# Block products in seven (Strassen's scheme) for two matrix products of a four-layer graph kernel, softmax steps moved forward, and layer 2 cut into pieces

## The chip, the cores and the metric

The kernel runs on one core of a Trainium2 chip. The metric is the device time of one execution in microseconds (us). Engines: PE is TensorE's matmuls, PEld its weight loads, DVE is VectorE, ACT is ScalarE, POOL is GpSimd.

## The reference, cut to what matters

`x` has shape (128 batches, 128 nodes, 256 features); `adj` is 128 x 128; all is fp32. Four layers follow one another, each wrapped in `x = layernorm(x + layer(x))`.

```python
# layer 0: graph attention over 512 edges (src, dst), 4 heads
Xq = (H @ W_lin.T).reshape(bt, n, h, dh)          # "queries"
Xv = (H @ W_val.T).reshape(bt, n, h, dh)
e  = einsum(leaky_relu(Xq[:, src] + Xq[:, dst]), a) + log(A0[src, dst] + EPS)
attn = softmax of e over the edges with the same src      # segment max, exp, sum
Y  = segment_sum(attn * Xv[:, dst], src) @ W_out.T
# layer 1: three products with weights, each mixed over nodes with adj * adj
h = relu(mix(x @ W1)); h = relu(mix(h @ W2)); out = mix(h @ W3)    # widths 512, 1024, 256
# layer 2: three matrices adj_0 (diagonal), adj_1, adj_2 (triangles), each with its own W[k]
# layer 3: mix, x @ W1.T, batch norm over all rows, relu, @ W2.T, batch norm
```

## The kernel before

The batches go in 32 groups of four. The main loop is a software pipeline: in repetition `k`, layer 2 and the first half of layer 3 work on group `a = k-1`, layer 1 on `c = k`, the end of layer 0 and the start of layer 1 on `b = k+1`, scores and softmax on `e = k+2`, and queries and values on `g = k+3`. Each engine's instructions stand in the order of the program, and the DVE lines in the prediction show DVE working them off in that order (a scaled copy at 1003.51, the three passes of a score from 1003.85, a sum at 1007.50, the next scaled copy at 1008.09). Layer 1's second product and layer 3's hidden product are already done in seven block products.

Queries and values of one batch are two matmuls of 512 columns, eight in a group; layer 1's first product has the same form:

```python
def values(k, i, copy=None, queue=None):
    ...
    pq = ps("pq")
    for c in range(DC):                                   # DC = 2
        nc.tensor.matmul(pq, s.xts[i // 2][:, i % 2, c, :], wqv[:, c, :], start=(c == 0), stop=(c == DC - 1))
    nc.scalar.copy(s.qt[:, i, :], pq[:, :D])
    copy(s.xv[:, i, :], pq[:, D:])

def first(k, i):
    ...
    for dc in range(DC):
        nc.tensor.matmul(ph, s.mx[i // 2 * 2][:, i % 2, dc, :], w1_sb[:, dc, :], ...)
    nc.scalar.activation(h1, ph, AF.Relu)
```

Layer 2 of one group. `mix` makes one batch's three mixed inputs: two by matmul, copied by ACT, and the diagonal one as a scaled copy by DVE. `prod` multiplies them with the weights. `behind` is the score of chunk 0, three passes of DVE over 1024 columns:

```python
mix(0); mix(1)
...
prod(0)
mix(2)
if behind:
    behind()                     # score(e, 0)
prod(1)                          # ends with a DVE sum of batches 0 and 1
mix(3)
layer_norm(wk, s.xr[:, 0:2, :])
prod(2); prod(3)                 # prod(i) reads mix(i)
```

The softmax is a chain of two scans, a subtraction and exponential, and two more scans (`softmax_parts`, a generator). Its steps stand between the products of the hidden layer; the last one stands behind layer 0's norm, just ahead of `attention`, whose transposes on PE read it:

```python
            next(parts, None)                 # last of layer 3's hidden products, and their statistics
            next(steps, None)                 # third scan
            gather(g)
            stage_a(b)                        # W_out, sum, layer 0's norm
            next(steps, None)                 # fourth scan
            third(c, 0)
            attention(e)                      # PE transposes the softmax result
```

Of the kernel before, what the change touches and what calls it, by code (L numbers as in the profile page):

```python
# [25 lines left out]
def gnn_stack(ctx: ExitStack, tc: tile.TileContext, x, adj, w_qv_t, a, w_out_t, src, dst,  # L26
# [101 lines left out]
    with ExitStack() as phase:  # L128
# [4 lines left out]

        quads = [Quad() for _ in range(NQ)]
# [49 lines left out]
        def values(k, i, copy=None, queue=None):  # L184

            copy = copy or nc.vector.tensor_copy
            s = quads[k]
            if i == 0:
                s.qt = wk.tile([P, QB, D], F32, tag="xb", name=f"qt{k}", bufs=1)
                s.xv = ws.tile([P, QB, D], F32, tag="xv", name=f"xv{k}", bufs=3)  # L190
            pq = ps("pq")
            for c in range(DC):
                nc.tensor.matmul(pq, s.xts[i // 2][:, i % 2, c, :], wqv[:, c, :], start=(c == 0), stop=(c == DC - 1))  # L193
            nc.scalar.copy(s.qt[:, i, :], pq[:, :D])
            copy(s.xv[:, i, :], pq[:, D:])
            if i == QB - 1:
                s.qd = q_dram[k % 4]
                (queue or nc.sync).dma_start(s.qd, s.qt.rearrange("p b d -> p (b d)"))

        def gather(k, z=None):  # L200

            s = quads[k]
            s.z = z or [ws.tile([P, QB * D], F32, tag="zs", name=f"zs{k}_{c}", bufs=NE) for c in range(NE)]
            jobs = [(t, c) for t in range(2) for c in range(NE)]
            if k == 0:
                jobs = [(0, 0), (0, 1), (1, 0), (0, 2), (1, 1), (0, 3), (1, 2), (1, 3)]
            for t, c in jobs:
                idx, op = ((src_idx, ALU.bypass), (dst_idx, ALU.add))[t]
                nc.gpsimd.indirect_dma_start(out=s.z[c], out_offset=None, in_=s.qd,  # L209
                                             in_offset=bass.IndirectOffsetOnAxis(ap=idx[:, c:c + 1], axis=0),  # L210
                                             compute_op=op)
# [14 lines left out]
        def softmax_parts(k):  # L226
# [12 lines left out]
            e = wk.tile([R, E], F32, tag="e", name="e", bufs=1)  # L239
            nc.vector.tensor_sub(e, pe[:R, :], m)  # L240
            nc.scalar.activation(e, e, AF.Exp)
            yield
            nc.vector.tensor_tensor_scan(f, keep_f, e, initial=0.0, op0=ALU.mult, op1=ALU.add)
            yield
            nc.vector.tensor_tensor_scan(m[:, ::-1], keep_b[:, ::-1], f[:, ::-1], initial=0.0,
                                         op0=ALU.mult, op1=ALU.max)
            s.ex, s.den = e, m
# [21 lines left out]

        def by_row(k, j, copy=None):  # L270

            s = quads[k]
            if j == 0:
                s.adc = wk.tile([P, R, N], F32, tag="adc", name=f"adc{k}", bufs=1)
# [34 lines left out]
        def mix1(k, j):  # L309
# [8 lines left out]
            if j == 0:  # L318
                s.mx = {}
                s.h1 = {}  # L320
                s.m2 = m2_tile()
            s.mx[j] = mx

        def first(k, i):
# [7 lines left out]
            s.h1[i] = h1  # L332


# [5 lines left out]
        def m2_tile():  # L340
            return wk.tile([P, 7, 2, 2, N], F32, tag="m2", name="m2", bufs=1)

        def mix2(k, i):
# [3 lines left out]
            for c in range(K1):  # L347
                nc.tensor.matmul(pm[:, c // 2, c % 2, :], s.h1[i][:, c * P:(c + 1) * P], wt_t, start=True, stop=True)  # L348
# [13 lines left out]
        def second_sums():  # L362

            a11, a12 = w2_sb[:, :2, :512], w2_sb[:, 2:, :512]
            a21, a22 = w2_sb[:, :2, 512:], w2_sb[:, 2:, 512:]
            s1, s2, s4 = (w2_s[:, i] for i in range(3))
            nc.vector.tensor_add(s1, a21, a22)
            nc.vector.tensor_sub(s2, s1, a11)
            nc.vector.tensor_sub(a21, a11, a21)
            nc.vector.tensor_sub(s4, a12, s2)  # L370
            second.blocks = {"A11": a11, "A12": a12, "A22": a22, "S1": s1, "S2": s2, "S3": a21, "S4": s4}
# [89 lines left out]
        def third(k, j, between=None):  # L461
            s = quads[k]
            p3 = ps("p3")
            for t in range(2):
                if t and between:
                    between()
                for f in range(K2):
                    nc.tensor.matmul(p3[:, t * D:(t + 1) * D], s.h2[f // 2][:, f % 2, j + t, :], w3_sb[:, f, :],  # L468
                                     start=(f == 0), stop=(f == K2 - 1))
            s3 = temp("s3")  # L470
# [21 lines left out]
        def stage_e(k, late=None, behind=None):  # L492
# [31 lines left out]
            if late is not None:  # L524
                late_sums(late)
            prod(0)
            mix(2)
            if behind:
                behind()
            prod(1)  # L530
            mix(3)
            layer_norm(wk, s.xr[:, 0:2, :])
            prod(2)
            prod(3)
# [18 lines left out]
        def hidden_sums():  # L553

            a11, a12, a21, a22 = (l3w1[:, h, o * 256:(o + 1) * 256] for o in range(2) for h in range(2))
            s1, s2, s3, s4 = (l3w1_s[:, i] for i in range(4))
            nc.vector.tensor_add(s1, a21, a22)
            nc.vector.tensor_sub(s2, s1, a11)
            nc.vector.tensor_sub(s3, a11, a21)
            nc.vector.tensor_sub(s4, a12, s2)  # L560
            hidden.blocks = {"A11": a11, "A12": a12, "A22": a22, "S1": s1, "S2": s2, "S3": s3, "S4": s4}
# [5 lines left out]
        def hidden(k):  # L567

# [4 lines left out]
            b11, b12, b21, b22 = (s.ag[h][:, o * half:(o + 1) * half] for h in range(2) for o in range(2))  # L573
            t12 = temp("t12")
            t1, t2, t3, t4 = t12[:, :half], t12[:, half:], s.spare[0], s.spare[1]
            nc.vector.tensor_sub(t1, b12, b11)
            nc.vector.tensor_sub(t2, b22, t1)
            nc.vector.tensor_sub(t3, b22, b12)
            nc.vector.tensor_sub(t4, b21, t2)

            def product(bank, blk, rhs, new):
                for i in range(2):
                    nc.tensor.matmul(bank[:, i, :], hidden.blocks[blk][:, i * P:(i + 1) * P], rhs,
                                     start=new and i == 0, stop=i == 1, skip_group_check=True)

            def bank(name):
                return ps(name).rearrange("p (i n) -> p i n", i=2)

            def kept_copy(src_, name):
                t = temp(name).rearrange("p (i n) -> p i n", i=2)  # L590
                nc.scalar.copy(t, src_)
                return t

            def block(row, col):
                return zt[:, 2 * row:2 * row + 2, col * half:(col + 1) * half]

            def stats(row):
                for c in (2 * row, 2 * row + 1):
                    nc.vector.bn_stats(st1[:, c, k, :], zt[:, c, :])

            yield
            y = bank("y3")
            product(y, "A11", b11, True)
            p1 = kept_copy(y, "p1")
            z = bank("z3")
            product(z, "S1", t1, True)
            yield
            product(y, "S2", t2, False)
            u2 = kept_copy(y, "u2")
            x = bank("x3")  # L610
            product(x, "A12", b21, True)
            nc.vector.tensor_add(block(0, 0), x, p1)
            yield
            product(y, "S3", t3, False)
            u3 = kept_copy(y, "u3")
            nc.vector.tensor_add(block(1, 1), z, u3)
            yield
            product(y, "A22", t4, False)
            nc.scalar.copy(block(1, 0), y)
            product(z, "S4", b22, False)  # L620
            nc.vector.tensor_add(block(0, 1), z, u2)
            stats(1)
            stats(0)
# [17 lines left out]
        w1_sb = ctile([P, DC, F1], "w1", pool=cst2)  # L641
        w2_sb = ctile([P, K1, F2], "w2", pool=cst2)
# [16 lines left out]

        def iteration(k):  # L660
# [4 lines left out]
            if a > 0:  # L665
                stage_e(a, c if has_c else None, (lambda: score(e, 0)) if has_e else None)
            else:
                late_sums(c)
                score(e, 0)
                hidden_sums()  # L670
# [11 lines left out]
            if has_g and g + 1 < NQ:  # L682
                quads[g + 1].xg = load_x(g + 1, "xg", 1, ws)
            stage_f(a)
            steps = softmax_parts(e) if has_e else iter(())
# [4 lines left out]
            parts = hidden(a)  # L690
            next(parts)
            if has_g:
                values(g, 0, nc.scalar.copy)
                values(g, 1, nc.scalar.copy)
            next(parts)
            next(steps, None)
            if has_g:
                values(g, 2, nc.scalar.copy)
            next(parts)
            next(steps, None)  # L700
            if has_g:
                values(g, 3, nc.scalar.copy)
            next(parts)
            if has_b:
                aggregate(b)
            next(steps, None)
            next(parts, None)
            next(steps, None)
# [5 lines left out]
            third(c, 0)  # L714
# [3 lines left out]
            if has_b:  # L718
                third(c, 2)
                third_mix(c, 0)  # L720
                mix1(b, 0)
                third_norm(c, 0)
            else:
                third(c, 2, lambda: third_mix(c, 0))
                third_norm(c, 0)
            third_mix(c, 2)
            if has_b:
                mix1(b, 2)
                first(b, 0)
            third_norm(c, 2)  # L730
            if has_b:
                firsts(b)

        def firsts(b):
# [536 lines left out]
```

## Time and profile before

| | before |
|---|---|
| time, median | 3290.4 us (3289.6 to 3292.4, 4 runs) |
| PE busy | 3178.6 us, 97% of the span |
| DVE, ACT, POOL busy | 59%, 38%, 20% |
| one repetition of the steady loop | 90.25 us |

How to read the lines: in a timeline a line gives the start in us, the duration of the merged group, engine, line of the program, operation, output <- inputs by name, shapes, and count; a bracket at its end gives the idle time of the engine just before the group and what ended it. Durations of neighbouring PE groups overlap, since the profile models the end of a matmul (in the prediction's lines one group ends at 1003.24 + 2.75 = 1005.99, and the next starts at 1005.83); so costs are taken from starts. The list of waits gives who waited for what: total us, times, longest. The lines themselves stand in the prediction.

### The profile page before, as it was taken

The numbers are of one execution on the slowest core, as the hardware profiler recorded it, in microseconds if no ns is written. First come the engines' busy times: TensorE is split into PE (matmuls) and PEld (weight loads), VectorE is DVE, ScalarE is ACT, GpSimd is POOL, SyncE is SP. The second block draws the span as 40 slices with busy tenths as digits, with TensorE's granted clock in tenths as the row PEclk, the third lists the DMA queues.
The fourth block names the chain that finished last, engine by engine and source line by source line (L and its number), as shares of the span: only waits on it lengthen the run. The fifth ranks groups of instructions, "written<-read, shape, count | busy, mean of one in ns | idle before, by whom it ended". The sixth has DMA issues, their size and how long they took to land. (4 is left out here: it accounts for less than half of the span.)

```text
span 3287.6 us, 39593 instructions
## 1 busy us (share of the span) xinstructions
PE 3178.6 (97%) x15176; PEld 2462.7 (75%) x15176; DVE 1955.8 (59%) x3779; ACT 1236.2 (38%) x2248; POOL 653.8 (20%) x541
## 2 busy tenths in 40 slices
PE   6899999999999999999999999999999999999997
PEld 3677887777787878877777878788777778883444
DVE  6655565555556555655555565556555556337878
ACT  2333333333333333333333333333333333325668
POOL 4201222222111112222222111122222220001225
PEclk7999999999999999999999999999999999999999
DMA  7612333333332223333333322233333331004457
GB/s 222 180 48 82 103 97 103 103 97 103 84 103 86 77 82 97 98 102 103 97 103 85 102 88 81 77 97 103 97 103 97 103 85 51 20 20 173 177 184 279
DMA packets 118748, 344.75 MB, mean 105 GB/s; under 512 B 15008, under 2 KB 51744, under 8 KB 110240
## 3 DMA queue, kind: packets, MB, share of 16 engines
q0 software_dynamic: 45552, 151.55, 18.2%
q1 hardware_dynamic: 70960, 188.71, 15.9%
q8 instruction: 120, 1.97, 0.2%
q10 hardware_dynamic: 2048, 1.97, 0.2%
q14 instruction: 68, 0.56, 0.1%
HBM read 256.20 MB, written 85.98 MB: 104 GB/s over the span
## 5 line engine op out<-in xcount | busy, mean ns | idle before, releaser
L388 PE MATMUL ph<-m,w 128*128 128x256 f32 x2048 | 463.2, 379 | 0.0
L209 POOL DMA_INDIRECT zs<-qd,src_idx x124 | 121.2, 978 | 1683.2 <-DMA qd<-qt 1639.5
L468 PE MATMUL p<-w,h 128*128 128x256 f32 x2048 | 455.3, 380 | 0.0
L468 PEld LDWEIGHTS p<-w,h 128*128 128x128 f32 x2048 | 386.6, 190 | 52.6 <-issue 0.5
L388 PEld LDWEIGHTS ph<-m,w 128*128 128x128 f32 x2048 | 386.7, 190 | 51.3
L388 PE MATMUL ph<-m,w_s 128*128 128x256 f32 x1536 | 352.4, 379 | 0.0
L516 PE MATMUL po<-l2w,ms 128*128 128x256 f32 x1536 | 348.1, 380 | 1.2 <-DVE ms L508 1.2
L388 PEld LDWEIGHTS ph<-m,w_s 128*128 128x128 f32 x1536 | 291.8, 190 | 39.7
L516 PEld LDWEIGHTS po<-l2w,ms 128*128 128x128 f32 x1536 | 284.9, 190 | 36.3 <-DVE ms L508 1.4
L193 PE MATMUL pq<-wqv,xt 128*128 128x512 f32 x512 | 237.3, 599 | 0.2 <-ACT xt L181 0.2
L328 PE MATMUL ph<-w,mx 128*128 128x512 f32 x512 | 235.9, 593 | 0.9 <-ACT mx L317 0.9
L209 POOL DMA_INDIRECT zs<-qd,dst_idx x124 | 205.7, 1659 | 119.7 <-DMA zs<-qd,src_idx 96.8
L112 ACT ACTIVATE ln_sd<-ln_mv,eps 128x2 f32<-128x2 f32 x192 | 56.5, 294 | 421.2 <-DVE ln_mv L107 421.2
L265 POOL DMA_INDIRECT attd<-at,att_idx x128 | 128.1, 1001 | 416.9 <-DMA attd<-at,att_idx 294.0
L401 DVE TENSOR_TENSOR h<-ph,u 128x512 f32<-128x512 f32 x128 | 88.2, 690 | 168.9 <-PE ph L388 115.2
L481 DVE TENSOR_TENSOR xr<-xr,po 128x512 f32<-128x512 f32 x64 | 43.7, 683 | 230.1 <-PE po L479 230.1
L348 PEld LDWEIGHTS pm<-wt_t,h 128*128 128x128 f32 x1024 | 131.8, 191 | 49.6 <-issue 38.7
L395 ACT COPY u<-ph 128x512 f32<-128x512 f32 x128 | 75.1, 586 | 242.9 <-PE ph L388 242.9
L504 ACT COPY ms<-pm 128x512 f32<-128x512 f32 x128 | 74.9, 586 | 237.6 <-PE pm L502 230.9
L193 PEld LDWEIGHTS pq<-wqv,xt 128*128 128x128 f32 x512 | 93.7, 193 | 84.3 <-issue 81.3
L221 DVE TENSOR_TENSOR zs<-zs,a_bc 128x1024 f32<-128x1024 f32 x124 | 151.9, 1225 | 4.2
L222 DVE TENSOR_REDUCE es<-zs 128x16 f32<-128x1024 f32 x124 | 151.3, 1220 | 4.3
(250 smaller groups left out, 5163.4 us busy)
## 6 DMA issues: line engine op xcount, KB each, us to landing
ad<-attd SPq DMA_DIRECT2D x32, 1024.0 KB, 4.7
zd<-z SPq DMA_DIRECT2D x31, 1024.0 KB, 7.0
zl<-zd SPq DMA_DIRECT2D x62, 512.0 KB, 3.5
xr<-in_x_dram SPq DMA_DIRECT2D x32, 512.0 KB, 5.8
x3d<-xr SPq DMA_DIRECT2D x32, 512.0 KB, 2.6
x3l<-x3d SPq DMA_DIRECT2D x32, 512.0 KB, 5.0
out_dram<-x3l POOLq DMA_DIRECT2D x31, 512.0 KB, 5.2
qd<-qt SPq DMA_DIRECT2D x30, 512.0 KB, 2.6
```

The costliest lines, as they stand in the source:

```text
L193: nc.tensor.matmul(pq, s.xts[i // 2][:, i % 2, c, :], wqv[:, c, :], start=(c == 0), stop=(c == DC - 1))
L209: nc.gpsimd.indirect_dma_start(out=s.z[c], out_offset=None, in_=s.qd, in_offset=bass.IndirectOffsetOnAxis(ap=idx[:, c:c + 1], axis=0), com ...
L221: nc.vector.tensor_mul(z3, z3, a_bc.unsqueeze(1).to_broadcast([P, QB, D]))
L222: nc.vector.reduce_sum(s.es[:, c, :], z.rearrange("p (r d) -> p r d", d=DH), axis=AX.X)
L265: nc.gpsimd.indirect_dma_start(out=ad, out_offset=bass.IndirectOffsetOnAxis(ap=att_idx[:, c:c + 1], axis=0), in_=s.at[:, c, :], in_offset= ...
L328: nc.tensor.matmul(ph, s.mx[i // 2 * 2][:, i % 2, dc, :], w1_sb[:, dc, :], start=(dc == 0), stop=(dc == DC - 1))
L348: nc.tensor.matmul(pm[:, c // 2, c % 2, :], s.h1[i][:, c * P:(c + 1) * P], wt_t, start=True, stop=True)
L388: nc.tensor.matmul(bank[g][:, i].rearrange("p b n -> p (b n)"), wa[:, c, f:f + P], s.m2[:, blk_b, c].rearrange("p b n -> p (b n)"), start= ...
L395: nc.scalar.copy(to[g], y[g])
L401: nc.vector.tensor_add(block(g, row, col), bank[g], kept_[g])
L468: nc.tensor.matmul(p3[:, t * D:(t + 1) * D], s.h2[f // 2][:, f % 2, j + t, :], w3_sb[:, f, :], start=(f == 0), stop=(f == K2 - 1))
L516: nc.tensor.matmul(po[:, i % 2, :], mss[i][:, t, dc, :], l2w[:, t, dc, :], start=(n3 == 0), stop=(n3 == 3 * DC - 1))
```

## The change

Its intent: with fewer columns through PE, which is busy for 97% of the span and so bounds the kernel, and without PE's wait for the softmax, the time should fall. It has three parts.

1. Queries and layer 1's first product go in seven products of half-size blocks instead of eight, at the cost of sums on DVE and copies on ACT. In the code, `A11` to `B22` are the blocks of the two factors, `S1` to `S4` and `T1` to `T4` are sums of such blocks (those of the weights are made once, in repetition 0), `part` copies a partial result out of `y` by ACT, and `out` writes one block of the result, most often as the sum of a bank and such a copy.
2. The softmax steps come earlier: all are done before the hidden layer's statistics and layer 0's norm.
3. To fill PE while the sums of part 1 are made, layer 2 becomes a generator that is run in pieces, and layer 1's third product too. The score of chunk 0 is now issued behind `prod(1)`, the end of layer 2's third piece (`mix(0)` and `mix(1)` are the first, run a repetition earlier). Three gather buffers take the place of four; the fourth chunk is gathered behind that score.

```diff
+        class Seven:
+            def p1(self):
+                self.y = ps("y")
+                self.mm(self.y, "A11", "B11", True)
+                self.k1 = self.part(self.y, 0)
+            def p5(self):
+                self.z = ps("z")
+                self.mm(self.z, "S1", "T1", True)
+            def p2(self):
+                x = ps("x")
+                self.mm(x, "A12", "B21", True)
+                self.out(0, 0, x, self.k1)
+            def p6(self):
+                self.mm(self.y, "S2", "T2", False)
+                self.k2 = self.part(self.y, 1)
+            def p7(self):
+                self.mm(self.y, "S3", "T3", False)
+                self.k3 = self.part(self.y, 2)
+                self.out(1, 1, self.z, self.k3)
+            def p4(self):
+                self.mm(self.y, "A22", "T4", False)
+                self.out(1, 0, self.y, None)
+            def p3(self):
+                self.mm(self.z, "S4", "B22", False)
+                self.out(0, 1, self.z, self.k2)
... (sums_a, sums_b, node_blocks, node_product: each product is two matmuls of 256 columns)
@@ stage_e: layer 2
             mix(0)
             mix(1)
-            if late is not None:
-                late_sums(late)
+            yield
             prod(0)
+            yield
             mix(2)
-            if behind:
-                behind()
             prod(1)
+            yield
             mix(3)
             layer_norm(wk, s.xr[:, 0:2, :])
             prod(2)
+            yield
             prod(3)
@@ iteration: its start
+            next(parts, None)
+            next(parts, None)
+            if has_e:
                 score(e, 0)
+                gather_last(e)
+            for _ in parts:
+                pass
... (second product)
@@ iteration: queries, softmax and hidden layer
+            steps = softmax_parts(e) if has_e else iter(())
+            next(steps, None)
+            h = hidden(a, room[5:] + room[2:4])
             if has_g:
-                values(g, 0, nc.scalar.copy)
-                values(g, 1, nc.scalar.copy)
+                run(q.p1, q.p5, q.p2)
+                next(steps, None)
+                q.p6()
+            run(h.p1, h.p5)
             next(steps, None)
             if has_g:
-                values(g, 2, nc.scalar.copy)
+                q.p7()
+            run(h.p2, h.p6)
             next(steps, None)
             if has_g:
-                values(g, 3, nc.scalar.copy)
+                run(q.p4, q.p3)
+                spill(g)
+            next(steps, None)
+            h.p7()
             if has_b:
                 aggregate(b)
+            run(h.p4, h.p3)
+            hidden_stats(a)
... (layer 0's end; third product)
@@ iteration: layer 1's first product
+            mix1(b, 0)
+            mix1(b, 2)
+            third_mix(c, 0)
+            next(rest)                        # a quarter of the third product
+            w = first_seven(b)
+            third_norm(c, 0)
+            next(rest)
+            run(w.p1, w.p5, w.p2)
+            next(rest)
+            w.p6()
+            next(rest, None)
+            w.p7()
+            third_mix(c, 2)
+            w.p4()
+            w.p3()
+            third_norm(c, 2)
+            quads[c].layer2 = stage_e(c)
+            next(quads[c].layer2)
```

## The prediction

One paragraph of the recorded text is cut where it is marked. No term of the forecast's sum stood in it: the terms still add up to -35.6 us, and 3290.7 - 35.6 = 3255 us. The durations behind the added work beside PE are those of the trace before: sums on DVE of 256 and 512 columns take 425 ns (L576) and 692 ns (L612), copies on ACT 0.37 to 0.38 us (L194, L195) and 0.59 us (L591), the table load 1.28 us (L241). "DVE's FIFO as traced" means the order of the DVE lines shown there, with 3.65 us of scoring ahead of the copy that PE wants.

> **What bounds the kernel now.** I read the head of the page first, then TensorE's waits, then the timelines of TensorE (PE) and VectorE (DVE) over one repetition of the steady loop. The head of the page:
>
> ```profile
> PE 3178.6 (97%) x15176; PEld 2462.7 (75%) x15176; DVE 1955.8 (59%) x3779; ACT 1236.2 (38%) x2248; POOL 653.8 (20%) x541
> PE   6899999999999999999999999999999999999997
> ```
>
> PE is busy nearly everywhere, and DVE, the next engine, has 40% to spare. So only two things pay: fewer columns through PE, and PE's remaining waits. The list of PE's waits names the largest one:
>
> ```profile
> PE pat L255 <- DVE m L245: 32.0, 31, 1.9
> PE py L289 <- ACT adc L275: 9.9, 1, 9.9
> PE pe L231 <- DVE es L224: 9.6, 1, 9.6
> ```
>
> The first comes once per group of four batches: the transposes of the softmax result wait for its last scan. The others come once, before the loop. Stage F (L547) of successive repetitions starts 90.25 us apart (946.90, 1037.15, 1127.40 us); of these PE idles only 0.99. From the PE timeline:
>
> ```profile
> 1003.24 2.75 PE L516 MATMUL po<-l2w,ms 128*128 128x256 f32 x12
> 1005.83 1.03 PE L502 MATMUL pm<-split_t,xr 128*128 128x256 f32 x4
> 1006.70 0.38 PE L507 MATMUL pt<-ident,xr 128*128 128x128 f32 x2
> 1006.91 5.34 PE L516 MATMUL po<-l2w,ms 128*128 128x256 f32 x24
> 1012.10 5.34 PE L388 MATMUL ph<-m,w 128*128 128x256 f32 x24
> ...
> 1038.93 3.60 PE L193 MATMUL pq<-wqv,xt 128*128 128x512 f32 x8
> 1042.37 1.03 PE L583 MATMUL y<-ag,l3w 128*128 128x256 f32 x4
> ...
> 1066.23 0.42 PE L255 MATMUL pat<-ident,m 16*128 16x16 f32 x4 [0.99 <-DVE m L245]
> ```
>
> Starts give costs; durations overlap. Eight records of 512 columns take 1042.37 - 1038.93 = 3.44 us. Each program matmul is two records (512 records here for 32 x 8 matmuls), so one costs 0.860 us. In layer 1's second product, 24 records of 256 columns take 5.18 us (1012.10 to the next group's 1017.28): 0.432 us per matmul. Cost follows columns. The weight load (190 ns a record) fits under a 256-column record (216 ns), so halving the width costs nothing.
>
> DVE in the same stretch:
>
> ```profile
> 1003.51 0.42 DVE L508 TENSOR_TENSOR ms<-pt,diag_bc 128x256 f32<-128x256 f32 x1 [2.00 <-PE pt L507]
> 1003.85 1.22 DVE L219 SCALAR_TENSOR_TENSOR zs<-zs 128x1024 f32<-128x1024 f32 x1
> 1005.10 1.23 DVE L221 TENSOR_TENSOR zs<-zs,a_bc 128x1024 f32<-128x1024 f32 x1
> 1006.36 1.22 DVE L222 TENSOR_REDUCE es<-zs 128x16 f32<-128x1024 f32 x1
> 1007.50 0.68 DVE L520 TENSOR_TENSOR xr<-xb,po 128x512 f32<-128x512 f32 x1
> 1008.09 0.42 DVE L508 TENSOR_TENSOR ms<-pt,diag_bc 128x256 f32<-128x256 f32 x1
> ```
>
> DVE works here in the program's order: layer 2's scaled copy of batch 2, the whole score of one chunk (3.65 us), the sum of batches 0 and 1, the scaled copy of batch 3. That copy ends at 1008.51; PE wants it for batch 3's product at 1006.91 + 2.59 = 1009.50. There is a margin of one microsecond.
>
> [...]
>
> **The change part by part.**
>
> *Seven block products.* Queries and layer 1's first product each go from 8 matmuls of 512 columns (8 x 0.860 = 6.88 us) to 7 x 2 of 256 (14 x 0.432 = 6.04): 0.84 saved. Queries change for groups 4 to 31 (28; the start keeps the plain form), the first product for groups 1 to 31 (31). 59 x 0.84 = 49.6 us, all on PE and so on the path.
>
> *Softmax earlier.* The last scan now comes before the hidden layer's statistics and layer 0's norm. Counting with row durations from the end of the second product: scans at 2.5, 6.0, 11.0 and 12.8 us, the last done near 14, while its transposes are due near 26.6. The 0.99 us wait goes in 29 repetitions: 28.7 us.
>
> *Added work beside PE.* Per repetition two times four sums of 256 columns (1.7 us) and three sums of 512 (2.07): 7.5 us more DVE. ScalarE: eight copies of 0.375 become four of 0.586, and three copies of 0.586 are added: 1.1 us more. DVE goes from 51.2 in 88.3 us to an estimated 66%. No new bound, but new places where PE can wait. In the queries' chain I find none: S1 is ready near 1.2 us, its product due at 3.1; the narrowest point (q.p3, which needs z read, behind the exponential's 1.28 us table load) has some 0.3 us. In layer 1's chain, S1 is ready 1 us early; the last ReLU comes some 0.1 us before the mixing that reads it, because layer 2's first two mixes stand between. I allow 0.1 us a repetition, 3 us.
>
> *Layer 2 cut into pieces.* This is where I expect a new wait. score(e,0) stood between mix(2) and prod(1) on DVE; now it stands after prod(1). So DVE first waits for prod(1)'s end (call it 0), adds at 0.27 (the same lag as 1012.10 to 1012.37 in the traces), starts scoring at 0.86, finishes at 4.51, and only then makes batch 3's scaled copy, until 4.93. PE: mix(3) 1.08, prod(2) 2.59, so prod(3) is due at 3.67 and starts near 4.98. New wait: 1.31 us, in repetitions 2 to 29 (28): 36.7 us. Before, DVE used its idle time during prod(1) for the score.
>
> *Edges.* The last three repetitions have no queries between the hidden layer's products, and p7 follows p6 directly: it waits for ScalarE's copy, some 0.85 us each. Repetition 0 loses its waits at the transposes (4.39 + 1.89) in part and gets a wait before mix2. Net about +3.
>
> Sum: -49.6 - 28.7 + 36.7 + 3 + 3 = -35.6; 3290.7 - 35.6 = 3255 us. The steady period should be about 88.9 us, from 90.25.
>
> **The rivals.** *No new wait* (PE comes late to prod(3) for another reason, or DVE reaches the score in time): then -49.6 - 28.7 + 6, 3218 us, 2.2% faster. For it: the author plainly placed pieces to fill gaps. Against it: the program order, and DVE's FIFO as traced. *DVE becomes the bound in stretches*: nodes' sums, norms and ReLUs of one chain queue behind each other, and PE loses another half to one microsecond in the queries or in layer 1: 3270 to 3285 us. For it: margins of 0.1 to 0.3 us; against it: 34% of DVE stays free. *Transfers*: the fourth chunk's gather is issued only after score 0, with three buffers in place of four. It is issued some 14 us before its score is due, when the transfer engines are nearly idle (DMA share 0.11 in the second product, 0.94 where gathers now crowd), so I expect nothing.
>
> **Range and chances.** The main term I doubt is the 36.7 us. All of it away: 3218. Half a microsecond more per repetition: 3271. So 3228 to 3272 in 8 of 10. Over 2% faster needs under about 3226 us: 0.16, nearly all from the first rival. Slower by 2% would take 4 us a repetition: 0.02.
>
> **What would show it.** Stage F's starts 88.9 us apart, not 90.25 and not 87.6; the wait at the pat transposes gone; a wait of PE at layer 2's product on DVE's scaled copy, 1.3 us in 28 repetitions; records of L193 and of the first product replaced by twice 14 matmuls of 256 columns per repetition at 0.432 us. Wrong would be: that new wait absent, or PE waits at the S1, p3 or p7 products, or at mix2, above 0.3 us per repetition, or waits on the gathers' transfers.

## The result, and the profile after

The changed kernel takes 3252.2 us (median; 3249.8 to 3254.3, 4 runs) against 3290.4. The ratio is 0.9883 (95% interval 0.9865 to 0.99): 1.2% less.

The head of the page after, and the largest entries in the list of PE's waits after:

```profile
PE 3137.4 (96%) x15884; PEld 2590.5 (80%) x15884; DVE 2145.3 (66%) x4200; ACT 1276.3 (39%) x2229; POOL 644.1 (20%) x541
```

```profile
PE po L666 <- DVE ms L658: 33.9, 29, 1.5
PE pe L356 <- DVE es L349: 10.7, 1, 10.7
```

PE is busy for 41 us less (waiting changes this figure too: e1 does the same 15884 records in 3127.3 us), DVE has gone to 66%. The wait at the softmax transposes (31 times) is gone from the top, and a wait at layer 2's product (L666) on DVE's scaled copy (L658) stands there, of the same size. PE's timeline of the steady loop shows all three parts of the change:

```profile
1028.33 1.03 PE L280 MATMUL y<-wqv,xt 128*128 128x256 f32 x4
1029.20 1.03 PE L280 MATMUL z<-wqv,m 128*128 128x256 f32 x4
...
1052.97 0.41 PE L379 MATMUL pat<-ident,f 16*128 16x16 f32 x4
1053.24 0.40 PE L379 MATMUL pat<-ident,m 16*128 16x16 f32 x4
...
1066.67 1.03 PE L280 MATMUL y<-w_s,adc 128*128 128x256 f32 x4
1067.57 1.12 PE L629 MATMUL po<-s,wt_t 128*128 128x512 f32 x2
1068.53 1.03 PE L280 MATMUL y<-w_s,mx 128*128 128x256 f32 x4
...
1082.27 1.03 PE L652 MATMUL pm<-split_t,xr 128*128 128x256 f32 x4
...
1083.35 2.76 PE L666 MATMUL po<-l2w,ms 128*128 128x256 f32 x12
1087.26 2.86 PE L666 MATMUL po<-l2w,ms 128*128 128x256 f32 x12 [1.16 <-DVE ms L658]
1089.95 5.34 PE L535 MATMUL ph<-m,w 128*128 128x256 f32 x24
```

A block product of the queries takes 0.87 us from start to start. The second softmax transposes follow the first with no bracket. And prod(3), due at 1083.35 + 2.59 = 1085.94, starts at 1087.26, 1.32 us late. DVE in the same stretch says why:

```profile
1079.87 0.42 DVE L658 TENSOR_TENSOR ms<-pt,diag_bc 128x256 f32<-128x256 f32 x1 [1.19 <-PE pt L657]
1082.54 0.69 DVE L670 TENSOR_TENSOR xr<-xb,po 128x512 f32<-128x512 f32 x1 [2.24 <-PE po L666]
1083.14 1.22 DVE L344 SCALAR_TENSOR_TENSOR zs<-zs 128x1024 f32<-128x1024 f32 x1
...
1085.65 1.22 DVE L347 TENSOR_REDUCE es<-zs 128x16 f32<-128x1024 f32 x1
1086.79 0.41 DVE L658 TENSOR_TENSOR ms<-pt,diag_bc 128x256 f32<-128x256 f32 x1
```

DVE stood idle for 2.24 us until prod(1) had ended, then summed, then scored for 3.65 us, and only then made the copy that PE wanted. Before the change the scoring filled that idle time (1003.85 to 1007.58, with the sum next at 1007.50, in the prediction's lines).

Where the 35.4 us between the two profiled spans (3287.6 and 3252.2) went: the stage F starts of repetitions 1 and 29 are 2527.18 us apart before and 2488.70 after, 38.5 us less (the steady period falls from 90.25 to 88.89). The rest of the span is 3.1 us longer, which says little: in e1 and e9, two runs of one kernel, that rest is 761.65 and 766.22 us.

### The profile page after: what moved, and what is told of

The parts are those of the page before. It is cut to its first block, busy times and chain, and to the rows that moved or that the text cites. A ratio compares the mean times of both kernels' runs of the same rounds, so it can differ in the third digit from the quotient of the medians.

```text
span 3252.2 us, 41204 instructions
## 1 busy us (share of the span) xinstructions
PE 3137.4 (96%) x15884; PEld 2590.5 (80%) x15884; DVE 2145.3 (66%) x4200; ACT 1276.3 (39%) x2229; POOL 644.1 (20%) x541
## 5 line engine op out<-in xcount | busy, mean ns | idle before, releaser
L616 PE MATMUL p<-w,h 128*128 128x256 f32 x2048 | 462.3, 379 | 0.0
L666 PE MATMUL po<-l2w,ms 128*128 128x256 f32 x1536 | 355.7, 382 | 33.9 <-DVE ms L658 33.9
L666 PEld LDWEIGHTS po<-l2w,ms 128*128 128x128 f32 x1536 | 282.7, 190 | 78.7 <-DVE ms L658 45.4
L329 POOL DMA_INDIRECT zs<-qd,dst_idx x123 | 192.5, 1565 | 258.2 <-DMA zs<-qd,src_idx 246.9
L344 DVE SCALAR_TENSOR_TENSOR zs<-zs 128x1024 f32<-128x1024 f32 x123 | 149.5, 1215 | 2.4 <-DMA zs<-qd,dst_idx 2.4
L120 DVE TENSOR_SCALAR xr<-xr,ln_mv,ln_rs 128x256 f32<-128x256 f32 x384 | 145.1, 420 | 6.9
L105 DVE BATCH_NORM_STATS2 ln_st<-xr 128x6 f32<-128x256 f32 x384 | 144.2, 417 | 5.5
L477 DVE TENSOR_TENSOR h<-z,adc 128x512 f32<-128x512 f32 x62 | 41.9, 675 | 153.9 <-ACT adc L471 153.8
L640 POOL TENSOR_TENSOR xb<-xr,bias 128x512 f32<-128x512 f32 x64 | 81.6, 1275 | 293.1 <-DVE xr L120 155.2
```

Source lines behind the costliest of these rows:

```text
L105: nc.vector.bn_stats(st[:, i, :], r[:, i, :])
L120: nc.vector.tensor_scalar(r[:, i, :], r[:, i, :], mv[:, i, 0:1], rs[:, i:i + 1], op0=ALU.subtract, op1=ALU.mult)
L329: nc.gpsimd.indirect_dma_start(out=s.z[c], out_offset=None, in_=s.qd, in_offset=bass.IndirectOffsetOnAxis(ap=idx[:, c:c + 1], axis=0), com ...
L344: nc.vector.scalar_tensor_tensor(z, z, SLOPE, z, op0=ALU.mult, op1=ALU.max)
L616: nc.tensor.matmul(p3[:, t * D:(t + 1) * D], s.h2[f // 2][:, f % 2, j + t, :], w3_sb[:, f, :], start=(f == 0), stop=(f == K2 - 1))
L640: nc.gpsimd.tensor_add(s.xb[:, j:j + 2, :], xj, bias.unsqueeze(1).to_broadcast([P, 2, D]))
```

## The experiments

The theory is that of the prediction: the gain is an eighth of the columns and the softmax wait, and half of it is given back by the place of one score in DVE's queue. Rivals: DVE is simply fuller (66%), and the wait would come up anywhere; the block form itself costs less or more than its columns; the gather of the last chunk matters. Each kernel was correct. They ran on three chips (e1 to e4, e5 to e7, e8 and e9), each with the kernel before beside them (medians 3290.8, 3291.3 and 3293.4 us); the ratios are to these. The steady period is read from stage F's starts, and is what the runs are compared by below.

| run | time, median us | ratio to before (95%) | steady period us |
|---|---|---|---|
| before | 3290.4 | 1 | 90.25 |
| changed | 3252.2 | 0.9883 (0.9865 to 0.9900) | 88.89 |
| e1 changed, score forward | 3213.2 | 0.9764 (0.9748 to 0.9780) | 87.47 |
| e2 before, score late | 3329.4 | 1.0119 (1.0102 to 1.0136) | 91.67 |
| e3 before, softmax ahead | 3256.6 | 0.9896 (0.9880 to 0.9913) | 89.10 |
| e4 before, half-width matmuls | 3293.1 | 1.0010 (0.9993 to 1.0028) | 90.33 |
| e5 changed, plain queries | 3276.5 | 0.9949 (0.9932 to 0.9965) | 89.72 |
| e6 changed, node sums twice | 3261.4 | 0.9908 (0.9892 to 0.9925) | 89.13 |
| e7 changed, score behind mix(3) | 3215.3 | 0.9765 (0.9749 to 0.9781) | 87.47 |
| e8 changed, plain first product | 3272.0 | 0.9936 (0.9920 to 0.9953) | 89.58 |
| e9 as e1, another chip | 3215.5 | 0.9758 (0.9742 to 0.9775) | 87.47 |

### e1: the score forward again, in the changed kernel

```diff
             mix(2)
+            yield
             prod(1)
             yield
```

(In repetition 0, where layer 2 runs without a score, one more `next(parts)` keeps the old order.)

> The changed kernel, with one more stop in layer 2's pieces so that the score of chunk 0 stands between mix(2) and prod(1) again, as in the kernel before; all else as changed. Theory (the order in VectorE's queue makes the wait at batch 3's product): the wait of PE on the scaled copy (33.9 us in 29 times in the changed kernel) goes, the start of batch 3's product moves forward by 1.32 us in 28 repetitions, steady period 88.89 - 1.32 = 87.57 us, time 3252 - 37 = 3215 us, 0.977 of before. Rival (VectorE simply has 7.5 us more work per repetition and the wait would come up elsewhere): the wait moves to another product, period stays within 0.3 us of 88.89 and the time above 3243 us.

Measured: 3213.2 us, ratio 0.9764, period 87.47. PE and DVE of this kernel at the same place:

```profile
1066.99 5.35 PE L666 MATMUL po<-l2w,ms 128*128 128x256 f32 x24
```

```profile
1063.86 1.22 DVE L344 SCALAR_TENSOR_TENSOR zs<-zs 128x1024 f32<-128x1024 f32 x1
...
1066.37 1.22 DVE L347 TENSOR_REDUCE es<-zs 128x16 f32<-128x1024 f32 x1
1067.51 0.68 DVE L670 TENSOR_TENSOR xr<-xb,po 128x512 f32<-128x512 f32 x1
1068.10 0.42 DVE L658 TENSOR_TENSOR ms<-pt,diag_bc 128x256 f32<-128x256 f32 x1
```

prod(2) and prod(3) run as one group of 24 records (L666) without a bracket, and the copy is ready at 1068.52, some 1.1 us before prod(3) is due (1066.99 + 2.59 = 1069.58). DVE does exactly the same work, so the rival of a full DVE falls. The gain is a little larger than expected, 1.42 us per repetition and not 1.32, since the group behind the wait is slower too: its 12 records took 2.69 us (1087.26 to 1089.95), and 12 without a wait take 2.59. Why is not shown, but the same 0.10 stands behind the shorter delays of e6 and e8 below.

### e2: the score late, in the kernel before

```diff
-            if behind:
-                behind()
             prod(1)
+            if behind:
+                behind()
```

> The kernel before, with nothing changed but the score of chunk 0 issued after prod(1) in place of ahead of it. Theory (order alone): PE gains a wait at batch 3's product of about 1.3 us in repetitions 2 to 29, period 90.25 + 1.31 = 91.56, time 3290.5 + 37 = 3327 us. Rival (the wait needs the added VectorE work of the seven-product form): no new wait, within 5 us of before.

Measured: 3329.4 us, ratio 1.0119, period 91.67, which is 1.42 longer. PE's waits of this kernel:

```profile
PE po L516 <- DVE ms L508: 33.6, 29, 1.2
PE pat L255 <- DVE m L245: 31.4, 31, 1.9
```

The new wait stands beside the old one, with none of the block products' sums on DVE. The order alone makes it, and it is worth the same 1.42 us in both kernels. So the changed kernel carried a loss of about 28 x 1.42 = 40 us that its other parts made up for.

### e3: the softmax ahead, in the kernel before

```diff
             parts = hidden(a)
             next(parts)
+            next(steps, None)
             if has_g:
                 values(g, 0, nc.scalar.copy)
...
             next(parts)
+            next(steps, None)
             if has_b:
                 aggregate(b)
-            next(steps, None)
             next(parts, None)
-            next(steps, None)
             if has_g:
                 gather(g)
```

> The kernel before, with nothing changed but each softmax step one or two places earlier, so that the last scan comes ahead of the hidden layer's statistics and layer 0's norm. Theory: the 0.99 us wait at the softmax transposes goes in 29 repetitions, period 89.26, time 3290.5 - 29 = 3261.5 us. Rival (earlier scans and exponential delay the copies that the hidden layer's products wait for): part of it comes back as waits at those products, time above 3275 us.

Measured: 3256.6 us, ratio 0.9896, period 89.10. PE's timeline of this kernel at the softmax transposes:

```profile
1054.99 0.41 PE L255 MATMUL pat<-ident,e 16*128 16x16 f32 x4
1055.26 0.39 PE L255 MATMUL pat<-ident,m 16*128 16x16 f32 x4
```

The edit does not do quite what the expectation says. The first three scans move up, the third ahead of the statistics, but the fourth and last stays behind layer 0's norm in the program. It still comes in time: the second transposes, which read it, start at 1055.26 with no bracket (above), and PE's wait for it falls from 32.0 us in 31 times to 2.3 in 2. So the run shows what the wait is worth, and not the changed kernel's own order, in which the last scan (1038.80) does come ahead of the statistics (1043.44).

The wait is gone and nothing took its place. The gain is 1.15 us per repetition, more than the 0.99 listed. The transposes show it: here the second group starts 0.27 us after the first; with the wait it started at 1066.23, 1.40 after the first (1064.83), which is 1.13 more. The bracket counts only from the modelled end of the group before (0.41 us after its start), not from the moment when PE could have started the next, 0.27 us after that start in this run.

### e4: the same columns in half-width matmuls, in the kernel before

```diff
-                nc.tensor.matmul(pq, s.xts[i // 2][:, i % 2, c, :], wqv[:, c, :], start=(c == 0), stop=(c == DC - 1))
+                for hf in range(2):
+                    nc.tensor.matmul(pq[:, hf * D:(hf + 1) * D], s.xts[i // 2][:, i % 2, c, :],
+                                     wqv[:, c, hf * D:(hf + 1) * D], start=(c == 0 and hf == 0), stop=(c == DC - 1),
+                                     skip_group_check=True)
```

(And the same in `first`.)

> The kernel before, with every 512-column matmul of the queries and of layer 1's first product issued as two of 256 columns with a weight load each: the same columns, twice the instructions. Theory (cost follows columns, the weight load of 190 ns hides under a record of 216): 64 x 8 x (2 x 0.432 - 0.860) = +2 us, time 3290 to 3295 us. Rival (twice the weight loads or the instructions cost something, so that the block form gains less than an eighth): 10 percent on 6.88 us in 64 uses, +44 us.

Measured: 3293.1 us, ratio 1.0010 with an interval that holds 1, period 90.33. PE's timeline of this kernel at the queries:

```profile
1041.68 3.62 PE L194 MATMUL pq<-wqv,xt 128*128 128x256 f32 x16
1045.13 1.03 PE L588 MATMUL y<-ag,l3w 128*128 128x256 f32 x4
```

Eight matmuls of 256 columns take 3.45 us where four of 512 took 3.44. In the trace before, a weight load takes 190 ns a record in the wide products (L388) and 141 to 142 in the transposes (L179, L507); a record of 256 columns takes 216 from start to start (0.432 us for two). Twice as many weight loads cost next to nothing: the period is 0.08 us longer, and 16 x (2 x 0.432 - 0.860) is 0.06. So the halved width takes nothing from the block form's gain.

### e5: the queries in the plain form, in the changed kernel

```diff
-                run(q.p1, q.p5, q.p2)
+                values(g, 0, nc.scalar.copy)
+                values(g, 1, nc.scalar.copy)
                 next(steps, None)
-                q.p6()
...
-                q.p7()
+                values(g, 2, nc.scalar.copy)
...
-                run(q.p4, q.p3)
-                spill(g)
+                values(g, 3, nc.scalar.copy)
```

> The changed kernel with the queries of groups 4 to 31 in the plain form again (8 matmuls of 512 columns, in the places of the seven products); layer 1's first product stays in seven. Theory (each use of the block form saves an eighth of its columns on PE and nothing else): 28 x 0.83 = +23 us on the changed kernel's 3252, that is 3275 us, period 89.72; the wait at batch 3's product stays at 1.16 us. Rival (the block form in the queries costs waits of its own, so that undoing it costs less): under +12 us.

(The sums of `queries` go too.) Measured: 3276.5 us, period 89.72, 0.83 longer than the changed kernel's, where the columns alone say 0.84. The wait at layer 2's product stays (33.6 us in 29 times). The queries' block form costs no wait of its own.

### e6: the node sums computed twice, in the changed kernel

```diff
             sums_a(a, a)
+            sums_a(a, a)
             return a
```

> The changed kernel with the four sums of node blocks computed twice over in each use of the block form (same values, same results): 1.6 us more of VectorE in two places of each repetition. Theory (VectorE is contiguous from the sums to the subtraction of the softmax, so there the 1.6 us pass on to the exponential and to ScalarE's third copy, which is due 0.3 us later; layer 1 has about 1.6 us to spare): PE waits some 0.5 us at q.p4 in 28 repetitions, nothing in layer 1, +10 to +20 us on 3252. Rival A (34 percent of VectorE is free, so it is hidden): under +4 us. Rival B (VectorE bounds those stretches): 2 x 1.6 x 28, about +90 us.

Measured: 3261.4 us, ratio 0.9908, period 89.13: 0.24 longer, some 7 us in all repetitions of the loop, and 8 to 9 by the ratios and the medians. This is a miss for each expectation, though nearest the theory. The place was right: the first line is the hidden layer's product ahead, the second is q.p4.

```profile
1036.56 1.03 PE L727 MATMUL y<-ag,l3w_s 128*128 128x256 f32 x4
1037.56 1.13 PE L281 MATMUL y<-wqv_s,xt 128*128 128x256 f32 x4
1038.52 1.03 PE L281 MATMUL z<-wqv,m 128*128 128x256 f32 x4
```

q.p4 is due 0.86 us after the group ahead, and comes after 1.00; it then takes 0.96 in place of 0.86. The delay is smaller than I worked out, since the exponential had not been waiting for DVE but for the load of its table. ACT of the changed kernel, then of this one:

```profile
1033.45 1.28 ACT L365 ACT_TABLE_LOAD   x1
1034.75 0.63 ACT L365 ACTIVATE f<-f 16x512 f32<-16x512 f32 x1
```

```profile
1034.77 1.28 ACT L366 ACT_TABLE_LOAD   x1
1036.41 0.63 ACT L366 ACTIVATE f<-f 16x512 f32<-16x512 f32 x1 [0.35 <-DVE f L365]
```

In the first the exponential starts as soon as the load is over (1033.45 + 1.28 = 1034.73), though DVE had been done since 1033.75; in the second DVE comes 0.35 us after the load. The load itself waits for DVE in neither: it starts 0.01 us after ACT's copy ahead has ended (1032.85 + 0.59 = 1033.44, and 1034.17 + 0.59 = 1034.76), before DVE's subtraction has ended. Counted from stage F's start (1026.11 and 1027.43), DVE's subtraction ends 1.31 us later in the second, the exponential starts 0.34 later, and PE loses 0.24. So most of the added work was hidden behind the load, and a quarter microsecond was not. The 34% of DVE that is free is not free at that point; one more round of sums there already costs 0.24 us a repetition.

### e7: the score behind mix(3), in the changed kernel

```diff
             prod(1)
-            yield
             mix(3)
+            yield
             layer_norm(wk, s.xr[:, 0:2, :])
```

> The changed kernel with the score of chunk 0 issued one step later still, behind batch 3's scaled copy instead of ahead of prod(1). Theory (what matters is only that no score stands between prod(1)'s sum and that copy in VectorE's queue): the wait goes as in the run that moved the score forward, period 87.5 us, time 3210 to 3218 us. Rival (the score is simply too late where it is, and later is worse, for the gather of the last chunk is issued behind it): a wait for the last chunk's score or for layer 2's norm, 3250 us or more.

Measured: 3215.3 us, ratio 0.9765, period 87.47: the same as e1. DVE of this kernel:

```profile
1069.83 0.42 DVE L658 TENSOR_TENSOR ms<-pt,diag_bc 128x256 f32<-128x256 f32 x1 [0.32 <-PE pt L657]
1070.18 1.22 DVE L344 SCALAR_TENSOR_TENSOR zs<-zs 128x1024 f32<-128x1024 f32 x1
```

The score comes even later than in the changed kernel (7.89 us after `prod(0)` starts, at 1062.29, against 7.14) and does no harm, nor does the gather of the last chunk, issued behind it. In the changed kernel DVE waits for a gather once in all, for 2.4 us before the steady loop, so that rival falls too. It is not the lateness of the score that costs; it is the score's place ahead of a copy that PE waits for.

### e8: layer 1's first product in the plain form, in the changed kernel

```diff
-            w = first_seven(b)
...
-            run(w.p1, w.p5, w.p2)
+            first(b, 0)
+            first(b, 1)
             next(rest)
-            w.p6()
+            first(b, 2)
             next(rest, None)
-            w.p7()
+            first(b, 3)
             third_mix(c, 2)
-            w.p4()
-            w.p3()
```

(Likewise in repetition 0.)

> The changed kernel with layer 1's first product of groups 1 to 31 in the plain form again (8 matmuls of 512 columns, spread over the places of the seven products); the queries stay in seven. Theory: what is left over of the steady period (90.25 before, less 1.155 for the softmax, less 0.825 for the queries, plus 1.42 for the late score, gives 89.69 against 88.89 measured) is this product's saving, 0.80 us in 31 uses: +25 us on 3252, about 3277 us, period 89.7. Rival (the wait for the last ReLU and the short delay at third_mix eat part of the gain): under +15 us, period under 89.4.

Measured: 3272.0 us, ratio 0.9936, period 89.58. The block form saves 0.69 us here, less than the 0.80 expected and the 0.84 of the columns; the time rises by 17 us (ratios) to 20 us (medians), between the theory's 25 and the rival's 15, so the rival is right in part. PE at `third_mix` of the second half in this kernel:

```profile
1071.82 1.02 PE L629 MATMUL po<-s,wt_t 128*128 128x512 f32 x2
1072.68 1.03 PE L652 MATMUL pm<-split_t,xr 128*128 128x256 f32 x4
```

It takes 0.86 us with no delay. In the changed kernel (shown above) it starts 0.90 after p7's start at 1066.67, so 0.04 late, and takes 0.96 from 1067.57: together 0.14. ACT's copy of the third product ends just before that start (1066.93 + 0.59 = 1067.52) and so comes just too late there. 0.84 less 0.14 is 0.70, which fits the 0.69.

### e9: e1 once more, on another chip

> The same kernel as the run that moved the score forward again, on another chip, to see that the version that beats both kernels holds: ratio to before 0.975 to 0.978, 3210 to 3218 us, steady period 87.47. A ratio above 0.98 would say that the first run owed something to its chip.

Measured: 3215.5 us, ratio 0.9758, period 87.47. The version that beats both kernels holds: 2.4% faster than before, with an interval that ends below 0.98 on both chips.

## Why the prediction was right

Predicted were 3255 us, in 3228 to 3272; measured were 3252.2. The predicted steady period of about 88.9 us was 88.89, though the prediction's own terms (2 x 0.84 + 0.99 - 1.31 - 0.1 = 1.26 less) give 88.99. The terms, one by one:

- **Cost follows columns** (0.432 us for 256 and 0.860 for 512 in the trace before). Predicted 0.84 us per use; the queries gave 0.83 (e5), the first product 0.69 (e8), since ACT's copy ahead of `third_mix` makes PE lose 0.14. The prediction had allowed 0.1 per repetition for another place, the last ReLU ahead of the second mixing; there PE does not wait (that ReLU ends at 1071.31 + 0.63 = 1071.94, the mixing starts at 1072.43). e4 shows that the halved width costs next to nothing (0.08 us a period).
- **The softmax wait.** Predicted 0.99, measured 1.15 (e3); in the changed kernel the two groups of transposes take 0.59 from start to start (1052.97 to 1053.56) and 1.75 before (1064.83 to 1066.58), 1.16 less. The mechanism was right and the term too small: the bracket starts at a modelled end.
- **The new wait.** Predicted: prod(3) starts 1.31 us late, in 28 repetitions. Measured: 1.32 late, but 1.42 lost per repetition (e1, e2), for the group behind the wait takes 0.10 longer. The cause, a score ahead of a wanted copy in DVE's queue, is shown from four sides: taken away in two ways (e1, e7), and made in the kernel before (e2), while changing the amount of other work on DVE does not move it (33.6 us in e5, 34.0 in e8, 33.9 in the changed kernel).
- **Work beside PE.** DVE at 66% was predicted and measured, though the added work was over-sized: a repetition holds 52.4 us of DVE before and 58.7 after, 6.3 more and not 7.5. The narrowest chain was named, the queries' behind the table load, with 0.3 us at q.p3; e6 found the edge one product earlier, at q.p4, for which ACT's copy is ready 0.26 us ahead (1035.29 + 0.56 = 1035.85, against 1036.11).
- **Edges.** Predicted about +3 us. The 3.1 us outside repetitions 1 to 28 do not test this: the prediction also has three uses of the first product and one softmax wait out there, so that its sum for that part is about 0, and e1 and e9 differ by 4.6 there. By the medians the gain is 38.3 us in all, as much as the 38.5 in the repetitions.

The terms measured apart give 90.25 - 1.15 - 0.83 - 0.69 + 1.42 = 89.00, against 88.89. The 0.11 left were not tested. Starts show three stages that differ by about as much: layer 1's second mixing took 0.89 + 0.89 + 1.90 = 3.68 us before and 3.57 after, the second half of its third product 7.01 and 6.90, its first mixing 1.79 and 1.89. In e8, which has the new order without this block form, the second mixing takes 3.58 too, so that difference comes with the order and not with the block form; why is not shown for any of the three.

The hit is thus partly luck in the small terms. Per repetition the prediction had 1.26 us, and 1.26 + 0.16 (softmax) - 0.11 (new wait) - 0.06 (block products) + 0.11 (not explained) = 1.36: two waits under-sized, with opposite signs. What decided the class, a gain of 1.2% and not of 2.4%, was the new wait, and that was read from the program's order and the durations in the trace.

## What to carry to other kernels

DVE worked its instructions off in the program's order in the traces here (in the changed kernel the score from 1083.14, then the copy at 1086.79). When a step moves in such an order, ask what stands behind it there and who waits for that: here three DVE passes (3.65 us) moved past one point, with no work added, cost 1.42 us per repetition, half of a gain won on the bottleneck. Put long work that nobody waits for either into the engine's idle time ahead of a wait (e1) or behind the copy that the bottleneck engine wants (e7), not between: the period was 87.47 us for each of these, and 88.89 with the score between. And take the cost of a wait of TensorE from starts, not from the listed idle time: a listed 0.99 us cost 1.15 per repetition (e3), a listed 1.16 cost 1.42 (e1, e2).
